# A four-layer macaron kernel: layer 1's second row of keys spread over its half steps, layer 2's expert weights turned ahead of layer 1, and the expert layer's first chunk placed beside the attention's end

## The chip, the core and the metric

The kernel runs on one core of a Trainium2 chip. A core has a matrix engine (TensorE, PE in the profile), a vector engine (VectorE, DVE), an engine for activations and copies (ScalarE, ACT), a general engine (GpSimd, POOL), a queue that issues transfers (SyncE, SP) and 16 DMA engines. Each engine takes its instructions from a queue of its own, in order, and waits on semaphores for the others. The metric is the device time of one execution in microseconds (us), lower being better.

## The reference

The whole model is a residual stream x of 1024 tokens (two rows of 512) with 256 features. Each of four layers is "half an FFN, an attention, half an FFN", each on a layernormed x. The parts that the change touches are the attention of layer 1, and the FFN of layer 2 that follows it:

```python
# layer 1 attention: keys are kept by importance, per row; 16 heads of 16
importance = (x @ Wi + bi)[..., 0]
threshold = sorted_desc[:, tidx][:, None]            # tidx = int(512 * 0.2) = 102
sparse_mask = maximum(importance > threshold, top_32)
q = (x @ Wq + bq)
k = (x @ Wk + bk) * mask
v = (x @ Wv + bv) * mask
out = softmax(q @ k / 4) @ v                          # a masked key keeps a zero score
x = x + out @ Wo + bo
...
# layer 1 FFN: x @ binarized(W).T + bias, taken half
# layer 2 FFN: eight experts, the best one of each token, its gate as weight
probs = softmax(xt @ wg)
out = onehot(argmax(probs)) * gate  combined over  einsum('nh,eoh->neo', xt, W) + b
x = x + 0.5 * out
```

## The kernel before

The kernel runs its stages one after the other: layer 0 with its routed experts, layer 1, and so on. Tokens are held as NC = 8 chunks of 128, four chunks (CB = 4) to a row; features as KD = 2 halves of 128. All operands are 32-bit floats. Matmuls are counted in passes in the trace, two passes to a matmul of this type. A tile framework writes the queues: it puts each engine's instructions in an order by its own estimates unless a block is wrapped in `in_order(tail, engines)` (line 230), which ties the listed engines' instructions to the order in which the code gives them. Tiles come from pools with a fixed number of buffers; a tile waits until the earlier holder of its buffer has been read. PSUM, which receives the matmuls' results, has eight banks.

**Layer 1** (`l1`, line 1382 on) keeps four banks for the scores (`score`). The other four are first one pool of four buffers (`a1m`), then four single buffers (`a1n`): t0 and t1 for transposed probabilities, o for the attention's output, and mm for everything else. Its steps:

- *Front.* `warm(psM, 18)` issues 18 matmuls on constants, 36 passes (L259). For each chunk, `pair` (L1424) adds two routed experts' results, which the y transfers (L861) bring; `sum_products` (L1430, ps_add) adds the rest, and `turn_x`, `back_products`, `back_out` do the half FFN; `measure` and `norm` the layernorm ahead of attention. After chunk 1, `bqs` (L1648), the scaled query bias, is computed on DVE.
- *Row 0's keys.* `importance` (L1474), `own`, `own_out` (L1488), then `ranks(b, cc)`: for one chunk, how many tokens stand above each of its tokens (L1494 on DVE and its sum L1495 on ACT) and which tie (L1498 on DVE). `places` (L1511, L1514) makes a 0/1 matrix from the ranks, `crowd` (L1557, px) multiplies by it so that at most 128 kept keys stand together, `crowded` (L1567) copies the result, `cut_product` and `cut_out` count those used. `key_products` and `keys_out` (L1580, L1592, L1595) make kT and its two masked copies kb; `value_products` and `vals_out` (L1606, L1610 to L1613) make va; `queries` (L1538) makes qT.
- *The prologue* (L1678 on), in order on PE, ACT and DVE: the row-1 importance, row 0's places, a `warm(psM, 4)`, `crowd(0)` and what follows, `queries(1, m)`, and the row-1 ranks.
- *The loop* over N = 16 half steps n (a chunk c = n // 2, and one half of the heads), L1811 on. `products(n)` (L1707, ps_s) makes scores; `lowered(n)` on DVE takes the row maxima (L1715) and subtracts them (L1717, p); `raised(n)` takes the exponential on ACT; `turn(n)` (L1727) transposes p on PE and evacuates it on ACT; `values(n)` (L1740, po) multiplies by va. One chunk behind follow `take_o`, `turn_o` (L1759), `divide`, `turn_back` (L1775), `project` (L1783, pw), `projected` (L1787), then the second half FFN: `centre_x`, `turn_fx` (L1798), `back_products` (L1453), `back_out` (L1456). In half steps n = 0 to 3 the loop also does row 1's places, crowd, keys and values; `kb(1)` is first used in products(8). After the last `lowered`, `self.lowered` marks that DVE instruction.

**Layer 2's weights** (`l2_weights`, L1855 on) load the eight experts' matrices (L1872, 8 transfers of 256 KB) and the gate and bias, and turn them with 32 transposes on PE (L1878) and eight 128x512 evacuations that alternate between DVE and ACT (`evac`, L225 and L227), in four PSUM buffers. This comes after layer 1 in the code; the framework puts it in gaps of the attention's last part. The big transfers use a shared pool of five weight buffers, tag "w", that layer 0's experts use as well.

**Layer 2's FFN** (`l2_ffn`, L1887 on), all experts for each chunk: `measure`, `turn` (L1932), `gates` (L1942, pl, and a chain of small DVE operations that gives the weights w), `experts(c, e2)` for e2 = 0 to 3 (L1964, ps_y, one whole bank of two experts' outputs, added to x by two DVE operations, L1969), `bias_turn`, `bias` (L1984) and `next_turn` (L1919). Only PE's instructions are held in order. All its PSUM tiles share one pool of eight buffers. It is called a second time later.

Of the kernel before, what the change touches and what calls it, by code (L numbers as in the profile page):

```python
# [18 lines left out]
P = 128  # L19
# [156 lines left out]
class Net:  # L176
# [1195 lines left out]
    def l1(self):  # L1372
# [12 lines left out]
        tidx = min(max(1, int(S * 0.2)), S - 1)  # L1385
        keep_min = 32
        assert max(tidx, keep_min) < P
        HQ = 32
        NQ = P // HQ
        GH = P // DH  # L1390
        NG = NH // NQ
        with ExitStack() as es:
# [132 lines left out]
            def cut_product(b):  # L1525
                nc.tensor.matmul(pxs[b][:, KD, 0:CB], self.ones, cuts[b], start=True, stop=True)
# [21 lines left out]

            pxs = {}

            def crowd(b):

                px = pxs[b] = psM.tile([P, KD + 1, P], F32, tag="mm", name="px")
                for k in range(KD):
                    for cc in range(CB):
                        c = b * CB + cc
                        nc.tensor.matmul(  # L1557
                            px[:, k, :],
                            xn[:, c, k * P : (k + 1) * P],
                            place[:, c, :],  # L1560
                            start=(cc == 0),
                            stop=(cc == CB - 1),
                        )
# [44 lines left out]
            def vals_out(b, xk):  # L1608
                uc = sbe.tile([P, 1], F32, tag="uc", name="uc", bufs=2)
                nc.vector.tensor_scalar(uc, self.c["icol"][:, 0:1], cuts[b], None, ALU.is_lt)  # L1610
                vt = sbe.tile([P, D], F32, tag="vt", name="vt", bufs=2)
                nc.vector.tensor_tensor(vt, pvs.pop(b), bv, ALU.add)
                nc.vector.tensor_scalar(  # L1613
                    vas[b][:, :, 0:DH], vt.rearrange("p (h d) -> p h d", h=NH), uc, None, ALU.mult
                )


            with tc.tile_pool(name="a1m", bufs=4, space=PSUM) as psM:
                self.pending.clear()
# [80 lines left out]
            st, po, outs = {}, {}, {}  # L1700

            def products(n):

                c, m = n // 2, n % 2
                for r in range(NQ):
                    q = slice(r * HQ, (r + 1) * HQ)
                    nc.tensor.matmul(  # L1707
                        score[:, r, m], qT[q, m, c * P : (c + 1) * P], kbs[c // CB][q, m], start=True, stop=True
                    )

            def lowered(n):
                c, m = n // 2, n % 2
                half = score[:, :, m]
                mh = mx[:, c, m * GH : (m + 1) * GH].rearrange("p (r j) -> p r j", j=2)
                nc.vector.tensor_reduce(mh, half, AX.X, ALU.max)  # L1715
                p = st[n] = sb.tile([P, NQ, 2, P], F32, tag="p", name="p", bufs=3)
                nc.vector.tensor_tensor(p, half, mh.unsqueeze(3).to_broadcast([P, NQ, 2, P]), ALU.subtract)  # L1717

            def raised(n):
                nc.scalar.activation(st[n], st[n], AF.Exp)  # L1720

# [87 lines left out]
                    f(k // 2)  # L1809

            with self.in_order({}):  # L1811
                products(0)
                lowered(0)
                for n in range(N + 6):
                    if n < N:
                        raised(n)
                    if n + 1 < N:
                        products(n + 1)
                    if n == 0:
                        places(1)  # L1820
# [12 lines left out]
                    if 0 <= n - 1 < N:  # L1833
# [3 lines left out]
                    within(turn_fx, n - 6)  # L1837
                    if n < N:
                        turn(n)
                    if n == 0:  # L1840
                        crowd(1)
                        cut_product(1)
                    elif n == 1:
                        key_products(1, xk)
                    elif n == 2:
                        value_products(1, xk)
                    within(turn_o, n - 2)
                    within(project, n - 3)
# [3 lines left out]
                        self.lowered = self.last_on("DVE")  # L1852


    @contextmanager  # L1855
    def l2_weights(self):

        nc, tc, a = self.nc, self.tc, self.a
        E = 8
        pre = "L2_ffn_"  # L1860
        with tc.tile_pool(name="f2keep", bufs=1) as keep:
            self.w8T = keep.tile([P, KD, E, D], F32, name="w8T")
            self.b8 = keep.tile([E, D], F32, name="b8")
            self.wg8 = keep.tile([P, KD, E], F32, name="wg8")
            self.into = keep.tile([P, KD, T], F32, name="nxT")
            nc.sync.dma_start(self.wg8, a[pre + "wg"].rearrange("(k p) e -> p k e", p=P))
            nc.sync.dma_start(self.b8, a[pre + "b"])
            with tc.tile_pool(name="f2pm", bufs=4, space=PSUM) as psM:
                for e0 in range(0, E, 4):
                    wn = self.w("w8")[:, : 4 * KD * D].rearrange("p (e c d) -> p e c d", e=4, c=KD)  # L1870
                    for e in range(4):
                        nc.sync.dma_start(wn[:, e], a[pre + "W"][e0 + e].rearrange("(c p) d -> p c d", p=P))  # L1872
                    for k in range(KD):
                        for e2 in range(0, 4, 2):
                            ps = psM.tile([P, 2, KD, P], F32, tag="mm", name="ps_w8")
                            for e in range(2):
                                for c in range(KD):
                                    nc.tensor.transpose(  # L1878
                                        ps[:, e, c, :], wn[:, e2 + e, c, k * P : (k + 1) * P], self.ident
                                    )  # L1880
                            self.evac(
                                self.w8T[:, k, e0 + e2 : e0 + e2 + 2, :].rearrange("p e d -> p (e d)"),
                                ps.rearrange("p e c d -> p (e c d)"),
                            )
            yield

    def l2_ffn(self):  # L1887

# [3 lines left out]
        with ExitStack() as es:  # L1892
            sb = es.enter_context(tc.tile_pool(name="f2", bufs=3))
            st = es.enter_context(tc.tile_pool(name="f2s", bufs=1))
            psM = es.enter_context(tc.tile_pool(name="f2m", bufs=8, space=PSUM))
            ms, xts, ws, wTs, nms = {}, {}, {}, {}, {}
            into, self.into = self.into, None
            self.turned = into
# [59 lines left out]
            def experts(c, e2):  # L1958
                if c < 0:
                    return  # L1960
                xT, w, xc = xts[c], ws[c], self.x[:, c, :]
                ps = psM.tile([P, 2, D], F32, tag="mm", name="ps_y")
                for k in range(KD):
                    nc.tensor.matmul(  # L1964
                        ps, xT[:, k, :], self.w8T[:, k, 2 * e2 : 2 * e2 + 2, :], start=(k == 0), stop=(k == KD - 1)
# [746 lines left out]
```

## Time and profile before

| | us |
|---|---|
| three runs: lowest, median, highest | 1840.1, 1843.48, 1847.05 |
| profiled execution | 1847.1 |
| its span in the trace | 1845.3 |
| busy in the span: PE, DVE, ACT, POOL | 1706.4, 1136.6, 808.8, 951.8 |
| layer 1's first warm-up pass on PE starts | 620.78 |
| first ps_add on PE | 630.23 |
| first products, second products | 686.18, 689.50 |
| last values product | 750.81 |
| layer 2 FFN's first transpose | 764.24 |

The page of the profile gives the busy time of each engine, and the same in slices. The timeline gives for every instruction or run of equal instructions on an engine its start, its duration, engine, line, operation, output and inputs, shapes and count, and in brackets the idle time of that engine before it with what ended the wait. The table of windows gives, for stretches of the span, how busy each engine was, the clock granted to PE (1.00 is full), and what the DMA engines did. Durations of matmuls in the trace include the pipeline's length, so two that follow each other overlap by a little.

### The profile page before, as it was taken

Reading aid. Unit: us, or ns where it says so; the run is one execution under the profiler, and the core shown is the slowest. Engines: PE = TensorE matmul, PEld = TensorE weight load, DVE = VectorE, ACT = ScalarE, POOL = GpSimd, SP = SyncE. Lnnn points to the kernel's source line nnn. Section 1 sums busy time; section 2 is a strip of 40 time slices with the busy share of each in tenths; the row PEclk is TensorE's granted clock in tenths of the full one; section 3 lists DMA queues with packets and bytes.
Section 4 is the critical chain, followed back from the end, with each engine's and each line's share of the span. In section 5 each row is a group of like instructions: output and inputs, shape, how many; then the busy total and the mean of one; then the engine's idle time right before and its main releaser. Section 6 shows DMA issues by size and latency. Waiting matters only on the chain. (4 is left out here: it accounts for less than half of the span.)

```text
span 1845.3 us, 29511 instructions
## 1 busy us (share of the span) xinstructions
PE 1706.4 (92%) x10342; PEld 1228.5 (67%) x10342; DVE 1136.6 (62%) x2945; ACT 808.8 (44%) x1399; POOL 951.8 (52%) x974
## 2 busy tenths in 40 slices
PE   6999989999999889998989898799999999999894
PEld 4677756666777657545655476577777777777573
DVE  5533358347433478776867534787777787778533
ACT  1122325421233136315631123678877777777121
POOL 4677646523777441202440263546756657767372
PEclk8999999999999999999989899899999999999897
DMA  9376551052665520102310133444445445443132
GB/s 295 107 229 188 164 193 37 20 176 56 189 182 182 186 75 1 47 1 82 108 33 12 40 103 115 159 140 166 154 140 176 158 140 172 161 149 127 37 117 94
DMA packets 122197, 226.52 MB, mean 123 GB/s; under 512 B 22398, under 2 KB 74988, under 8 KB 121894
## 3 DMA queue, kind: packets, MB, share of 16 engines
q1 hardware_dynamic: 97046, 179.08, 30.1%
q0 software_dynamic: 18944, 42.16, 7.3%
q10 hardware_dynamic: 6032, 3.10, 0.6%
q8 instruction: 91, 1.49, 0.3%
q14 instruction: 84, 0.69, 0.1%
HBM read 195.59 MB, written 41.81 MB: 129 GB/s over the span
## 5 line engine op out<-in xcount | busy, mean ns | idle before, releaser
L645 POOL DMA_INDIRECT xe<-table,sl_get x176 | 183.1, 1040 | 155.1 <-DVE sl_get L617 98.0
L673 PE MATMUL ps_gu<-we,xeT 128*128 128x352 f32 x704 | 225.1, 460 | 0.0
L704 POOL DMA_INDIRECT rows<-ye,sl_put x176 | 176.7, 1004 | 87.9 <-issue 40.2
L2200 DVE SCALAR_TENSOR_TENSOR xc<-pp,L_attn_cols,xc 128x511 f32<-128x511 f32 (+2 forms) x216 | 161.3, 748 | 25.8 <-ACT xc L2196 20.7
L698 PE MATMUL ps_ye<-we,hT 88*128 88x256 f32 x704 | 168.2, 379 | 2.9 <-ACT ye L227 1.6
L678 DVE SCALAR_TENSOR_TENSOR he<-se,xe,ps_gu 128x176 f32<-128x176 f32 x176 | 69.9, 397 | 158.6 <-ACT se L677 154.8
L673 PEld LDWEIGHTS ps_gu<-we,xeT 128*128 128x128 f32 x704 | 126.1, 190 | 55.3 <-DVE xeT L225 1.4
L698 PEld LDWEIGHTS ps_ye<-we,hT 88*128 88x128 f32 x704 | 133.1, 190 | 37.2 <-ACT ye L227 3.6
L2321 DVE SCALAR_TENSOR_TENSOR lm<-lm,jb,top 128x128 f32<-128x128 f32 x576 | 153.5, 342 | 0.0
L2403 POOL TENSOR_TENSOR y<-y,sg 128x512 f32<-128x512 f32 x72 | 91.9, 1276 | 103.5 <-DVE y L2402 102.2
L2433 PE MATMUL yacc<-wt,y 128*128 128x256 f32 x576 | 142.7, 391 | 0.6 <-DVE x L2451 0.3
L677 ACT ACTIVATE se<-ps_gu 128x176 f32<-128x176 f32 x176 | 55.9, 318 | 183.8 <-PE ps_gu L673 181.9
L2348 PE MATMUL pz<-lateT,wt 128*128 128x128 f32 x1024 | 126.2, 276 | 6.3 <-ACT xt L2291 4.1
L2341 POOL TENSOR_TENSOR ce<-ce,CT 128x1024 f32<-128x1024 f32 x54 | 128.0, 2371 | 0.0
L2348 PEld LDWEIGHTS pz<-lateT,wt 128*128 128x128 f32 x1024 | 120.3, 193 | 9.9 <-ACT xt L2291 5.3
L1964 PE MATMUL ps_y<-w8T,xT 128*128 128x512 f32 x256 | 125.0, 618 | 0.0
L2193 PE MATMUL pp<-lateT,wx 128*128 128x512 f32 x256 | 122.1, 600 | 0.8 <-DVE xc L2200 0.8
L2433 PEld LDWEIGHTS yacc<-wt,y 128*128 128x128 f32 x576 | 103.8, 190 | 22.8 <-issue 9.2
L2414 POOL TENSOR_TENSOR sqs<-sqs,sq 128x512 f32<-128x512 f32 x56 | 71.4, 1275 | 85.5 <-ACT sq L2413 85.5
L2376 PE MATMUL py<-lm,xt 128*64 128x128 f32 x1152 | 107.2, 279 | 6.9 <-PE pz L2348 2.1
L2333 DVE TENSOR_TENSOR lm<-lm,M 128x1024 f32<-128x1024 f32 x72 | 87.2, 1215 | 41.9 <-ACT lm L2326 39.4
L2193 PEld LDWEIGHTS pp<-lateT,wx 128*128 128x128 f32 x256 | 48.9, 192 | 57.4 <-issue 52.5
(520 smaller groups left out, 3519.6 us busy)
## 6 DMA issues: line engine op xcount, KB each, us to landing
lm<-rows SPq DMA_DIRECT2D x72, 512.0 KB
ce<-rows SPq DMA_DIRECT2D x54, 512.0 KB
y<-rows SPq DMA_DIRECT2D x16, 768.0 KB
we<-in_L_ffn_w_gate_dram SPq DMA_DIRECT2D x64, 176.0 KB
we<-in_L_ffn_w_up_dram SPq DMA_DIRECT2D x64, 176.0 KB
we<-in_L_ffn_w_down_dram SPq DMA_DIRECT2D x64, 176.0 KB
we<-in_L_ffn_w_dram SPq DMA_DIRECT2D x48, 176.0 KB
wx<-in_L_attn_in_proj_w_dram SPq DMA_DIRECT2D x16, 512.0 KB
```

Of the source, the lines that this page charges most:

```text
L645: nc.gpsimd.indirect_dma_start(xe[:, i, :], None, table, bass.IndirectOffsetOnAxis(get[:, at + j : at + j + 1], 0), bounds_check=T - 1, oo ...
L673: nc.tensor.matmul(pg, xeT[:, k, i * P : (i + 1) * P], wgu[:, :, k], start=(k == 0), stop=(k == KD - 1))
L698: nc.tensor.matmul(py[:, i, :], hT[:, q, i * P : (i + 1) * P], wd[:, q, :], start=(q == 0), stop=(q == 1))
L704: put_rows = nc.gpsimd.indirect_dma_start(rows, bass.IndirectOffsetOnAxis(put[:, at + j : at + j + 1], 0), y[:, i, :], None, bounds_check= ...
L1964: nc.tensor.matmul(ps, xT[:, k, :], self.w8T[:, k, 2 * e2 : 2 * e2 + 2, :], start=(k == 0), stop=(k == KD - 1))
L2193: nc.tensor.matmul(pp, wv[:, k, :], xT[:, k, b * S : (b + 1) * S], start=(k == 0), stop=(k == KD - 1))
L2200: nc.vector.scalar_tensor_tensor(out[:, 3 - w :], pp[:, : S - 3 + w], cw[:, m, w : w + 1], out[:, 3 - w :], ALU.mult, ALU.add)
L2321: nc.vector.scalar_tensor_tensor(k["lm"][:, h, :], k["lm"][:, h, :], jb[:, k["c"], n : n + 1], top, ALU.add, ALU.min)
L2341: nc.gpsimd.tensor_tensor(k["ce"], k["ce"], ct, ALU.mult)
L2348: nc.tensor.matmul(pz[:, m, :], u["wz"][:, kk, m * P : (m + 1) * P], xT[:, kk, c * P : (c + 1) * P], start=(kk == 0), stop=(kk == KD - 1),)
L2376: nc.tensor.matmul(py[i * HP : (i + 1) * HP, m, :], w[:, h * HP : (h + 1) * HP], v[:, h, :], start=(m == 0 and n == 0), stop=(n == len(src ...
L2433: nc.tensor.matmul(yacc[cc // 2][:, cc % 2, :], k["y"][:, m, :], u["wo"][:, m, :], start=(u["g"] == 0 and m == 0 and cc % 2 == 0), stop=(u ...
```

## The change

There are three parts.

1. The loads and turns of layer 2's expert weights move into a method `l2_turned()`, which `l1` calls before anything else. The pool that holds the turned weights stays open through layer 1. In the built program the 32 transposes stand on PE just ahead of the 18 warm-up matmuls; the 256 KB loads stand on SP behind the loads of layer 0's last experts; on DVE, `bqs` stands ahead of DVE's four evacuations.
2. In layer 1's prologue row 0's places and the first half of its crowd come ahead of `own(1)`, the `warm(psM, 4)` is gone, `crowded` copies on ACT, `products(0)` comes ahead of the queries of row 1, and `lowered(0)` is in the prologue. `ranks(1, 1..3)` move into half steps 0 and 1 (on DVE's queue `ranks(1, 1)` still stands between `ranks(1, 0)` and `keys_out(0)`; the other two come after `lowered(1)`). Row 1's places and crowd move from n = 0 to 2, its copy and cut from 1 to 3, its keys from 1 and 2 to 4, its values from 2 and 3 to 4 and 5. The two kb and the one va of row 1 move from DVE to POOL.
3. In layer 2's FFN the eight shared PSUM buffers become four (psM) and four (psY). The first chunk's ps_y takes psM, the other chunks' psY. In the built program PE's queue interleaves the first chunk's FFN with the attention's last steps: values(15), first half of pt(0), turn_fx(5), second half, turn_o(7), back_products(5), gates(0), half of ps_y(0,0), turn_back(7), its other half, project(7), pt(1), the first chunk's bias_turn, half of ps_y(0,1), turn_fx(6), the other half, back_products(6), gates(1), ps_y(0,2), turn_fx(7), bias(0), half of ps_y(0,3), back_products(7), the other half, and then ps_y(1,0).

The diff, cut to its core:

```diff
+        self.l2_turned()
...
-            def crowd(b):
+            def crowd(b, ks=range(KD)):
...
-                nc.vector.tensor_copy(xk, pxs[b][:, 0:KD])
+                nc.scalar.copy(xk, pxs[b][:, 0:KD])
...
-                    nc.vector.tensor_scalar(kbs[b][:, :, j, :], kT, self.c["own"][:, j : j + 1], None, ALU.mult)
+                    (nc.gpsimd if b else nc.vector).tensor_scalar(
+                        kbs[b][:, :, j, :], kT, self.c["own"][:, j : j + 1], None, ALU.mult
+                    )
...
-                nc.vector.tensor_scalar(
+                (nc.gpsimd if b else nc.vector).tensor_scalar(
                     vas[b][:, :, 0:DH], vt.rearrange("p (h d) -> p h d", h=NH), uc, None, ALU.mult
...
                     importance(1)
+                    places(0)
+                    crowd(0, [0])
                     own(1)
-                    places(0)
-                    self.warm(psM, 4)
-                    crowd(0)
+                    crowd(0, [1])
                     chosen(0)
                     own_out(1)
                     cut_product(0)
+                    xk = crowded(0)
                     ranks(1, 0)
-                    xk = crowded(0)
                     key_products(0, xk)
+                    cut_out(0)
                     value_products(0, xk)
-                    cut_out(0)
-                    ranks(1, 1)
                     keys_out(0, xk)
+                    products(0)
+                    vals_out(0, xk)
                     for m in range(KD):
                         queries(1, m)
-                    vals_out(0, xk)
-                    ranks(1, 2)
-                    ranks(1, 3)
+                    lowered(0)
...
-                products(0)
-                lowered(0)
                 for n in range(N + 6):
...
                     if n == 0:
+                        ranks(1, 1)
+                    elif n == 1:
+                        ranks(1, 2)
+                        ranks(1, 3)
+                    elif n == 2:
                         places(1)
                         chosen(1)
-                    elif n == 1:
+                    elif n == 3:
                         xk = crowded(1)
                         cut_out(1)
-                    elif n == 2:
-                        keys_out(1, xk)
-                    elif n == 3:
+                    elif n == 5:
                         vals_out(1, xk)
                     within(projected, n - 4)
                     within(divide, n - 3)
+                    if n == 4:
+                        key_products(1, xk)
+                        keys_out(1, xk)
...
-                    if n == 0:
+                    if n == 2:
                         crowd(1)
                         cut_product(1)
-                    elif n == 1:
-                        key_products(1, xk)
-                    elif n == 2:
+                    elif n == 4:
                         value_products(1, xk)
...
-            psM = es.enter_context(tc.tile_pool(name="f2m", bufs=8, space=PSUM))
+            psM = es.enter_context(tc.tile_pool(name="f2m", bufs=4, space=PSUM))
+            psY = es.enter_context(tc.tile_pool(name="f2y", bufs=4, space=PSUM))
...
-                ps = psM.tile([P, 2, D], F32, tag="mm", name="ps_y")
+                ps = (psY if c else psM).tile([P, 2, D], F32, tag="mm", name="ps_y")
```

`l2_turned` holds the body of the old `l2_weights` unchanged (loads, transposes, evacuations), but for the tile `nxT`, which `l2_weights` still makes, in a pool of its own.

More of the change, by code (lines that the diff above doesn't have):

```diff
@@ L1549, in l1 @@
             pxs = {}
-            def crowd(b):
-                px = pxs[b] = psM.tile([P, KD + 1, P], F32, tag="mm", name="px")
-                for k in range(KD):
+            def crowd(b, ks=range(KD)):
+                if b not in pxs:
+                    pxs[b] = psM.tile([P, KD + 1, P], F32, tag="mm", name="px")
+                px = pxs[b]
+                for k in ks:
                     for cc in range(CB):
@@ L1612, in vals_out, with products, lowered @@
                 nc.vector.tensor_tensor(vt, pvs.pop(b), bv, ALU.add)
-                nc.vector.tensor_scalar(
+                (nc.gpsimd if b else nc.vector).tensor_scalar(
                     vas[b][:, :, 0:DH], vt.rearrange("p (h d) -> p h d", h=NH), uc, None, ALU.mult
                 )
+            st, po, outs = {}, {}, {}
+            def products(n):
+                c, m = n // 2, n % 2
+                for r in range(NQ):
+                    q = slice(r * HQ, (r + 1) * HQ)
+                    nc.tensor.matmul(
+                        score[:, r, m], qT[q, m, c * P : (c + 1) * P], kbs[c // CB][q, m], start=True, stop=True
+                    )
+            def lowered(n):
+                c, m = n // 2, n % 2
+                half = score[:, :, m]
+                mh = mx[:, c, m * GH : (m + 1) * GH].rearrange("p (r j) -> p r j", j=2)
+                nc.vector.tensor_reduce(mh, half, AX.X, ALU.max)
+                p = st[n] = sb.tile([P, NQ, 2, P], F32, tag="p", name="p", bufs=3)
+                nc.vector.tensor_tensor(p, half, mh.unsqueeze(3).to_broadcast([P, NQ, 2, P]), ALU.subtract)
             with tc.tile_pool(name="a1m", bufs=4, space=PSUM) as psM:
@@ L1686, in l1 @@
                     cut_product(0)
+                    xk = crowded(0)
                     ranks(1, 0)
-                    xk = crowded(0)
                     key_products(0, xk)
+                    cut_out(0)
                     value_products(0, xk)
-                    cut_out(0)
-                    ranks(1, 1)
                     keys_out(0, xk)
+                    products(0)
+                    vals_out(0, xk)
                     for m in range(KD):
                         queries(1, m)
-                    vals_out(0, xk)
-                    ranks(1, 2)
-                    ranks(1, 3)
+                    lowered(0)
             psM = es.enter_context(tc.tile_pool(name="a1n", bufs=1, space=PSUM))
[L1700 to L1717, printed above, removed]
             def raised(n):
@@ L1852, in l1, with l2_turned @@
                         self.lowered = self.last_on("DVE")
-    @contextmanager
-    def l2_weights(self):
+    def l2_turned(self):
         nc, tc, a = self.nc, self.tc, self.a
@@ L1860, in l2_weights @@
         pre = "L2_ffn_"
[L1861 to L1885, printed above, removed]
@@ new lines, in l2_turned @@
+        self.l2es = ExitStack()
+        keep = self.l2es.enter_context(tc.tile_pool(name="f2keep", bufs=1))
+        self.w8T = keep.tile([P, KD, E, D], F32, name="w8T")
+        self.b8 = keep.tile([E, D], F32, name="b8")
+        self.wg8 = keep.tile([P, KD, E], F32, name="wg8")
+        nc.sync.dma_start(self.wg8, a[pre + "wg"].rearrange("(k p) e -> p k e", p=P))
+        nc.sync.dma_start(self.b8, a[pre + "b"])
+        with tc.tile_pool(name="f2pm", bufs=4, space=PSUM) as psM:
+            for e0 in range(0, E, 4):
+                wn = self.w("w8")[:, : 4 * KD * D].rearrange("p (e c d) -> p e c d", e=4, c=KD)
+                for e in range(4):
+                    nc.sync.dma_start(wn[:, e], a[pre + "W"][e0 + e].rearrange("(c p) d -> p c d", p=P))
+                for k in range(KD):
+                    for e2 in range(0, 4, 2):
+                        ps = psM.tile([P, 2, KD, P], F32, tag="mm", name="ps_w8")
+                        for e in range(2):
+                            for c in range(KD):
+                                nc.tensor.transpose(
+                                    ps[:, e, c, :], wn[:, e2 + e, c, k * P : (k + 1) * P], self.ident
+                                )
+                        self.evac(
+                            self.w8T[:, k, e0 + e2 : e0 + e2 + 2, :].rearrange("p e d -> p (e d)"),
+                            ps.rearrange("p e c d -> p (e c d)"),
+                        )
@@ L1887, in l2_ffn, with l2_weights @@
+    @contextmanager
+    def l2_weights(self):
+        with self.l2es:
+            with self.tc.tile_pool(name="f2into", bufs=1) as p:
+                self.into = p.tile([P, KD, T], F32, name="nxT")
+                yield
     def l2_ffn(self):
```

## The prediction

> **What bounds the kernel now.** The page's busy line comes first: TensorE (PE) is busy 92% of the 1845.3 us span, VectorE (DVE) 62%, GpSimd (POOL) 52%. The change touches only 617 to 780 us, so its worth is read from that stretch, in the table of windows (in each column busy us, the instruction count in brackets; then the granted clock, 1.00 being full, the DMA share, GB/s):
>
> ```profile
> 620.00:630.00 10.00, 9.22 (x35) 7.92 (x36) 2.36 (x2) 0.00 (x0) 2.33 (x7) 0.80 0.61 198
> 687.00:690.00 3.00, 0.50 (x4) 0.50 (x8) 2.93 (x6) 2.97 (x6) 0.00 (x0) 0.81 0.00 0
> 690.00:696.00 6.00, 6.00 (x35) 5.34 (x30) 2.95 (x6) 2.79 (x4) 0.00 (x0) 0.52 0.00 0
> 757.00:764.00 7.00, 5.31 (x27) 3.60 (x26) 4.17 (x12) 1.92 (x4) 3.44 (x8) 1.00 0.51 150
> 764.00:770.00 6.00, 5.25 (x11) 2.68 (x12) 2.39 (x12) 0.58 (x2) 0.79 (x2) 0.50 0.55 176
> ```
>
> There are three weak places. PE starts layer 1 at 0.80 of its clock; it stands idle for most of 687 to 690 and then works six us at 0.52; it is a quarter idle at the attention's end, and the next FFN then begins at 0.50. The change alters all three. The timeline (start, duration, what it is, in brackets the idle time before it and what ended that) shows each. First the start of layer 1:
>
> ```profile
> 620.78 9.61 PE L259 MATMUL warm<-cst 128*128 128x256 f32 x36 [4.55 <-PEq L839]
> ...
> 624.02 1.67 DVE L1648 TENSOR_SCALAR bqs<-col_L_attn_bq 128x2 f32<-128x2 f32 x1 [7.16 <-issue]
> 630.23 3.62 PE L1430 MATMUL ps_add<-y,cst 128*128 128x256 f32 x16
> ```
>
> The first pair sum (y, 0.69 from 627.29) is ready at 627.98, but ps_add stands behind the warm-up in PE's queue and starts at 630.23, with no idle time in front of it: PE bounds here, by idle work. Then the attention's start, PE's own rows:
>
> ```profile
> 678.21 1.95 PE L1557 MATMUL px<-place,xn 128*128 128x128 f32 x16
> ...
> 682.65 3.60 PE L1538 MATMUL pq<-xT,w 128*128 128x512 f32 x8
> 686.18 0.71 PE L1707 MATMUL ps_s<-kb,qT 32*128 32x256 f32 x8
> 689.50 1.23 PE L1707 MATMUL ps_s<-kb,qT 32*128 32x256 f32 x8 [2.61 <-DVE p L1717]
> 690.66 1.97 PE L1727 MATMUL ps_t<-cst,p 128*128 128x128 f32 x8
> 692.42 3.52 PE L1557 MATMUL px<-place,xn 128*128 128x128 f32 x16
> ```
>
> Ahead of them eight warm-up passes take 1.99 from 676.38. The same crowd matmuls (px) take 1.95 us at 678 and 3.52 at 692, after the idle 2.61. Later the loop is DVE's: in the window 710 to 720 DVE is busy 9.50 of 10 us, of which each half step's lowered() takes 1.23 + 1.23. And the end:
>
> ```profile
> 750.81 0.64 PE L1740 MATMUL po<-pT,va 128*32 128x128 f32 x16
> ...
> 764.24 0.69 PE L1932 MATMUL pt<-cst,xn 128*128 128x128 f32 x2 [0.58 <-DVE x L1456]
> 766.31 3.76 PE L1964 MATMUL ps_y<-w8T,xT 128*128 128x512 f32 x4
> ...
> 775.26 3.70 PE L1964 MATMUL ps_y<-w8T,xT 128*128 128x512 f32 x8
> ```
>
> From the last values product at 750.81 to the FFN's first transpose at 764.24 PE does remnants of attention and the 32 weight transposes. The next chunk's experts begin in the middle of the last row: 775.26 + half of 3.70 = about 777.0.
>
> **A, the weights turned early: a loss of 6.6 us.** The 32 transposes now stand ahead of the warm-up. The w8 loads are issued when experts 27 and 28 free their buffers, about 600, and land before 620; the two small loads go ahead of expert 4's weights on SP, issued at 447.15 and used at 469.9, so they hide (at 8 issues of 0.38 us the worst is 3, within those 20). PE is free at 620.78. A transpose pass costs 0.11 us at full clock (the row of 32 at the end) and 0.21 at half. The first 16 fill four PSUM buffers: 16 x 0.21 = 3.4, to 624.2. The fifth tile needs tile 0's buffer, whose evacuation is a DVE copy that the scheduler queues behind bqs. bqs ran 624.02 to 625.69, after the scatters; one 128x512 copy takes 0.69, so 626.4. The other 16 transposes run to 628.2 (1.76 at 0.11) or 629.9 (0.21). Then 36 warm passes at 0.213 (9.61 us held about 9 at 0.427 and 27 at 0.213): 7.7, up to 9.6 if the clock fell again. So ps_add starts at 635.9 to 639.0, against 630.23: 5.6 to 8.8 later, and I take 6.6, near the warm end. The floor is 3.5, the bare transposes at full clock, if the evacuations do not hold PE. Nothing later absorbs it: the front chunks follow each other every 3.54 us in a PE, DVE, POOL, DVE chain, and the data of y had landed.
>
> **B, the second row's keys later: a gain of 3.3 us.** Removed from PE: the warm 1.99 ahead of crowd(0). Walking each queue with the rows' durations: place(0) is done at 675.57, crowd(0), the importance product (0.4) and the cut products end near 677.9, ACT's copy takes 0.37 where DVE's took 0.42, key products 1.1, kT 0.62, kb 0.64: products(0) at about 681.4 instead of 686.18, since it no longer waits for queries(1) (3.60). lowered(0) ends near 684.7 and the queries fill PE while it runs, so products(1) comes at 685.3 instead of 689.50. That is 4.2 to 4.8. It is partly given back: ranks(1,2) and ranks(1,3), 2 x 1.2 us on DVE, move out of the time when PE did queries and into the loop that DVE bounds. For it the idle 2.61 goes, and with it the half clock (px 3.52 back to 1.95, ps_t 1.97 to 1.04: 2.5, of which DVE's own pace hides some). Moved to POOL and ACT are 2 kb x 0.35, va 0.35 and one later copy of 0.42. The walk reaches products(8) at 714.8 against 718.30, 3.5; I take 3.3. Ends: 1.4 if the clock falls as before, 4.8 if the whole head start is kept. kb(1) on POOL costs 2 x 0.93 by the nearest row (below) but is needed only at products(8), some 10 us later: nothing, or 1 if POOL were a whole chunk late.
>
> ```profile
> L2280 POOL TENSOR_SCALAR wt<-wt,L_attn_cols x8: 920/933/1086, 665.3 to 1141.5; 128x256 f32<-128x256 f32 x8
> L1498 DVE SCALAR_TENSOR_TENSOR cmp<-ib,imp,cst x8: 740/746/1215, 667.4 to 685.8; 128x512 f32<-128x512 f32 x8
> ```
>
> The second row (min/median/max ns) has one instruction of 1215, at 671.79, just beside a POOL addition; that is what POOL work beside the new in-loop ranks could do to DVE: 0.47 each, 1.4 for three, inside my ends. [...]
>
> **C, the FFN's first chunk beside the attention's end: a gain of 9.7 us.** In the changed order PE's queue holds, from values(15) to the second chunk's first ps_y: attention's values 0.6, four pairs of transposes 1.1, turn_o 0.4, projection 0.9, three back products 2.6, together 5.6; the chunk's 4 x 1.72 experts and 2.0 of pt, pl, ct, pb, 8.9. Sum 14.5, to 765.3 at best. The waits that stay are ACT's evacuations behind the one buffer mm (turn_back, project, turn_fx and back_products all use it) and DVE's adds; walking the queues in the new order gives 1.9 of them, so 767.2 instead of 777.0. The 32 transposes (3.5) and 8 evacuations are gone from here, and the FFN starts warm (its first tile 1.9, not 3.76). Gain 9.7; ends 8 (each of the eight DVE steps in the chain 0.2 later) and 11.7. What is late next is x(7), whose last addition moves from 764.18 to 767.0, but its FFN chunk comes 50 us later. The same walk with the old order puts the first transpose at 764.19, where the trace has 764.24. After that the order is the same, 8.47 us a chunk (pl at 772.38 and 780.84).
>
> [...]
>
> **Sum.** -6.6 + 3.3 + 9.7 = 6.4 us gained. The profiled execution took 1847.1 (span 1845.3 and 1.8 around it): 1840.7. It lies 3.6 above the median of the runs, 1843.48, from which 6.4 leaves **1837**. About 0.5% (9.2 us) is what a measurement here can tell from no change; faster is below 1834.3, slower above 1852.7.
>
> **Rivals.**
> - More is gained. If the evacuations run early and the clock holds, A costs 3.5 to 4.5; with B at 4.5 and C at 11 that is 11 to 12: 1832. For it: bqs is the only row that delays the evacuation. Against it: bqs waits for the scatters and stands ahead in DVE's queue.
> - The end does not overlap as intended: one mm buffer and DVE's statistics ahead of the additions stretch the chain, so C is 4: 1843. For it: the old chain of single-buffer steps took 13.4 us from 750.81 to 764.24 with PE only 5.31 of 7 busy. Against it: DVE is 4.17 of 7 busy there.
> - Slower: in the FFN the experts' tiles had eight shared PSUM buffers and now four. Each ps_y waits until the one a chunk earlier has been read. It decides once DVE lags PE by 8.47 - 1.72 = 6.7 us; the row at 777.28 (experts' sums, right behind their products at 777.0) lags under 1.3. The other tiles (pt, pl, ct, pb, pt_nx) have only four too. If either cost 1 us a chunk, over 16 chunks of two calls it is 16: 1853; it is slower from there on.
>
> **Chances.** Forecast 0.52, more gain 0.24, less overlap 0.16, four buffers 0.08. Faster: five sixths of the second, 0.20, and a tail of the first, 0.06: 0.26. Slower: 0.07 from the last. The rest, 0.67, is within 0.5%. The range: all ends good is 3.5 against 4.8 + 11.7, 1830.5; all ends bad 8.8 against 1.4 + 4, 1847. I keep 1829.5 to 1846.
>
> **What would show it.** A: ps_add starts about 6.6 us late with the warm-up right before it. B: no idle over 1 us before products(1), granted clock near 1.00 in the eight us after it, lowered() back to back. C: from values(15) to the second chunk's first ps_y 16.4 us instead of 26.2, clock 1.00, chunks still 8.47 apart. It is wrong if ps_y waits for DVE in the steady chunks, if the clock falls behind the turned weights, or if the in-loop ranks stretch the half steps by more than their 2.4 us.

## The result, and the profile after

The changed kernel takes 1848.03 us (median of 20 runs) against 1842.69 for the kernel before (20 runs): ratio 1.0026, interval 1.0015 to 1.0037, that is 2.8 to 6.8 us slower. A second set (12 runs, e5 below) gave 1.0017, 1.0004 to 1.0029. So it is within 0.5%, but on the other side of no change than forecast, and outside the range of 1829.5 to 1846. The profiled execution took 1847.55 (span 1845.7), as good as the 1847.1 of before's; two single executions do not show the difference, the runs do. So the stages are compared below, and more executions of both.

First the windows that were shown of before, and four others, in the changed kernel (busy us of PE, PEld, DVE, ACT, POOL with counts, then the granted clock, DMA share, GB/s):

```profile
620.00:630.00 10.00, 8.21 (x47) 7.16 (x46) 4.34 (x7) 1.76 (x3) 2.33 (x7) 0.93 0.90 317
660.00:670.00 10.00, 7.71 (x35) 5.26 (x34) 6.40 (x18) 1.12 (x3) 8.98 (x16) 0.79 0.00 1
670.00:680.00 10.00, 9.02 (x26) 4.92 (x24) 6.21 (x16) 3.66 (x9) 4.63 (x8) 0.70 0.01 2
687.00:690.00 3.00, 2.29 (x14) 1.16 (x13) 2.83 (x9) 0.00 (x0) 0.00 (x0) 1.00 0.00 0
690.00:696.00 6.00, 4.58 (x23) 2.12 (x21) 4.14 (x5) 4.61 (x7) 0.00 (x0) 1.00 0.00 0
757.00:764.00 7.00, 7.00 (x33) 4.51 (x32) 5.90 (x24) 2.02 (x7) 3.58 (x9) 1.00 0.00 1
764.00:770.00 6.00, 6.00 (x24) 3.79 (x23) 4.29 (x17) 0.58 (x2) 2.03 (x4) 1.00 0.00 0
830.00:840.00 10.00, 6.58 (x13) 2.67 (x12) 2.71 (x7) 1.43 (x3) 0.78 (x2) 0.66 0.00 0
840.00:850.00 10.00, 10.00 (x41) 6.94 (x40) 4.84 (x11) 1.95 (x5) 0.00 (x0) 0.66 0.00 0
```

Two of the three weak places are mended: full clock from 687 to 696, and PE busy without a break from 757 to 770. But there are new ones, at 660 to 680 and at 830 to 850, where the diff moves nothing. PE's start of layer 1:

```profile
617.23 3.65 PE L1883 MATMUL ps_w<-cst,w 128*128 128x128 f32 x16 [4.05 <-DVEq L839]
622.67 1.97 PE L1883 MATMUL ps_w<-cst,w 128*128 128x128 f32 x16 [1.79 <-DVE w8T L225]
624.48 7.93 PE L259 MATMUL warm<-cst 128*128 128x256 f32 x36
632.25 3.62 PE L1431 MATMUL ps_add<-y,cst 128*128 128x256 f32 x16
```

Sixteen transposes at half clock, 1.79 us of waiting for the evacuation on DVE, sixteen at full clock, the warm-up, and only then ps_add, 15.0 us after PE was free (9.45 before). Next POOL and PE around the last chunk of layer 1's front:

```profile
663.84 0.95 POOL L2292 TENSOR_SCALAR wt<-wt,L_attn_cols 128x256 f32<-128x256 f32 x1 [0.24 <-DVE ln_mv L294]
...
664.94 0.95 POOL L2292 TENSOR_SCALAR wt<-wt,L_attn_cols 128x256 f32<-128x256 f32 x1
665.85 0.57 POOL L303 TENSOR_TENSOR ln_rs<-ln_rs,mhalf 128x1 f32<-128x1 f32 x1
666.40 1.84 POOL L2292 TENSOR_SCALAR wt<-wt,L_attn_cols 128x256 f32<-128x256 f32 x2
```

```profile
664.21 1.13 PE L1454 MATMUL ps_y<-bwT,fxT 128*128 128x256 f32 x4
667.17 0.66 PE L1445 MATMUL pt<-cst,fxn 128*128 128x128 f32 x2 [1.84 <-DVE fxn L307]
```

The same place in the kernel before:

```profile
661.81 0.66 PE L1444 MATMUL pt<-cst,fxn 128*128 128x128 f32 x2 [0.38 <-DVE fxn L307]
...
665.34 3.83 POOL L2280 TENSOR_SCALAR wt<-wt,L_attn_cols 128x256 f32<-128x256 f32 x4
```

wt is a weight of layer 2's attention, scaled on POOL. Before, all four scalings stood behind the last chunk's ln_rs (665.34 on). Now two of them stand ahead of its last step at 665.85, inside the layernorm, and two right behind it, and PE waits 1.84 us for the result instead of 0.38. By the code, part 1 gives two of the shared weight buffers back early: wt is loaded at 646 instead of 658, and the framework puts the scaling earlier too. Then the attention's end, in PE's rows:

```profile
754.55 0.64 PE L1744 MATMUL po<-pT,va 128*32 128x128 f32 x16
...
758.86 1.10 PE L1976 MATMUL ps_y<-w8T,xT 128*128 128x512 f32 x2
...
769.80 2.74 PE L1976 MATMUL ps_y<-w8T,xT 128*128 128x512 f32 x6
```

The overlap is there: the second chunk's experts begin a third into the last row, at 770.7, 16.1 us behind values(15) (26.3 before). And the end of that FFN. There pt_nx turns the last chunk's normed x, pp and pd are the first products of layer 2's attention, pd with only 8 columns, and pst, some 39 us on, is the landmark used below. The idle time is older than the change; first the changed kernel, then the kernel before in the execution of e15:

```profile
833.63 0.69 PE L1931 MATMUL pt_nx<-cst,nxn 128*128 128x128 f32 x2 [2.96 <-DVE nxn L307]
834.78 6.17 PE L2205 MATMUL pp<-nxT,wb 128*128 128x512 f32 x8 [0.46 <-ACT nxT L1932]
840.79 4.63 PE L2145 MATMUL pd<-wb,nxT 128*128 128x8 f32 x32
```

```profile
835.84 0.44 PE L1919 MATMUL pt_nx<-cst,nxn 128*128 128x128 f32 x2 [2.97 <-DVE nxn L307]
836.73 3.70 PE L2193 MATMUL pp<-nxT,wb 128*128 128x512 f32 x8 [0.46 <-ACT nxT L1920]
840.27 3.63 PE L2133 MATMUL pd<-wb,nxT 128*128 128x8 f32 x32
```

The same idle time, the same matmuls, but pp takes 6.17 us instead of 3.70 and pd 4.63 instead of 3.63: half clock (0.66 in the windows above), 64 us behind the second chunk's first ps_y, from which the order is as before.

Stage by stage, in us, from traces that share these landmarks on PE (before and e15 are one kernel, changed and e5 another; e9, e10, e11 are told below):

| from - to | before | e15 | changed | e5 | e10 | e9 | e11 |
|---|---|---|---|---|---|---|---|
| PE free - first ps_add | 9.45 | 9.34 | 15.01 | 14.86 | 14.67 | 14.58 | 9.57 |
| - row 0's importance | 32.03 | 32.04 | 35.38 | 33.69 | 32.01 | 33.71 | 31.65 |
| - row 1's importance | 11.02 | 10.96 | 13.23 | 10.82 | 9.66 | 11.01 | 9.65 |
| - products(8) | 45.02 | 44.98 | 41.31 | 41.32 | 41.59 | 41.31 | 43.21 |
| - values(15) | 32.51 | 32.52 | 32.38 | 32.38 | 32.37 | 32.38 | 32.38 |
| - second chunk's ps_y | 26.27 | 26.24 | 16.11 | 16.12 | 16.12 | 16.12 | 16.12 |
| - last pt_nx | 63.14 | 63.14 | 63.24 | 63.23 | 63.14 | 63.20 | 63.20 |
| - first pst (layer 2's attention) | 38.66 | 38.65 | 45.30 | 45.21 | 44.38 | 38.65 | 38.64 |
| sum | 258.1 | 257.9 | 262.0 | 257.6 | 253.9 | 251.0 | 244.4 |

### The profile page after: what moved, and what is told of

Read it like the earlier page. It is cut to its first block, busy times and chain, and to the rows that moved or that the text cites. A ratio compares the mean times of both kernels' runs of the same rounds, so it can differ in the third digit from the quotient of the medians.

```text
span 1845.7 us, 29481 instructions
## 1 busy us (share of the span) xinstructions
PE 1708.8 (93%) x10334; PEld 1231.0 (67%) x10334; DVE 1134.2 (61%) x2940; ACT 808.5 (44%) x1401; POOL 953.4 (52%) x977
```

## The experiments

My theory after the first trace: the forecast's three terms hold, and two are missing, POOL's new order and more half clock. The rivals: the spread keys or the split buffers lose; or the half clock is luck, alike in both kernels. Runs e1 to e4 were made on a chip on which the kernel before takes 1932.2 us, the others where it takes 1841 to 1843; so whole times are compared as ratios alone. Stages that no edit touches read alike on both chips (products(8) to values(15) takes 32.51 us in e1's trace and in before's). The ratio is always to the kernel before on the same chip.

**e1: part 1 alone.** The kernel before with

```diff
+        self.l2_turned()        # in l1; l2_weights as in the changed kernel
```

> The kernel before with part 1 alone (weights turned ahead of layer 1, eight shared PSUM buffers and old key order kept). My theory: the loss of the change is made at the start of layer 1 (5.6 us later ps_add after PE is free, as in the changed kernel's trace) and by the four wt scalings of layer 2 that now stand on POOL inside the last layernorms (1.8 us and up to 2.2 of half clock behind it); the 32 transposes that go from the attention's end give back at most 3.5. So +4 to +8 us against before. Rival, that the loss comes from the spread keys or the FFN's split buffers: within 2 us of before.

Ratio 1.0047 (1.0023 to 1.0071), 9 us, with an interval of 4.4 to 13.7. Its stages: 14.45 to the first ps_add, then 35.39 and 13.18, where before has 9.45, 32.03, 11.02: 10.5 us lost; from values(15) to the second chunk 22.76 instead of 26.27, 3.5 won; from the last pt_nx to the first pst 42.04 instead of 38.66, 3.4 lost again to half clock. Together 10.4 lost in the trace, a little more than the 4 to 8 expected: part 1 is the loss.

**e2: part 2 alone.** The changed kernel's `l1` without that call, the rest as before.

> The kernel before with part 2 alone (prologue, keys spread, kb and va on POOL). My theory: the changed trace's gain between the second importance product and values(15), 3.8 us, is kept: -3 to -4 us against before. Rival, that the ranks and the second row's keys inside the DVE-bound loop cost more than the head start is worth: 0 to +4 us.

Ratio 1.0003 (0.9976 to 1.003). The expected gain was not found; from row 1's importance to values(15) it is 78.4 us, where before has 77.5. In its trace 6.8 us at half clock fall behind products(1), and products(1) to products(8) take 32.30 us; e3, with the same part 2, has no half clock there and takes 29.40. Its last stage, 44.38 instead of 38.66, holds half clock as the changed kernel's does, though nothing of layer 2 was touched. Whether part 2 by itself is worth anything is not settled by these runs.

**e3: part 1 undone.** The changed kernel with

```diff
-        self.l2_turned()        # in l1
...
     def l2_weights(self):
+        self.l2_turned()
```

> The changed kernel with part 1 undone: the weights are loaded and turned behind layer 1 in the code, as before. My theory: without the loss at the start (5.6) and on POOL (2 to 4) it keeps the 3.8 of the keys and a part of the overlap at the end, some 3 of 10: -5 to -8 us against before, 10 to 13 below the changed kernel. Rival (the start is hidden or the loss is elsewhere): at or above before.

Ratio 0.9949 (0.9922 to 0.9977), 10 us below before on that chip. 10.19 to the first ps_add and 31.82 to row 0's importance: both losses are gone; 21.28 at the end instead of 16.11.

**e4 and e10: POOL's order.** The changed kernel with the scalings held behind the last layernorm of the front:

```diff
+            self.fronts = self.last_on("Pool")       # ahead of the loop's pools in l1
...
+                        with tc.issue_after(self.fronts):
                             nc.gpsimd.tensor_scalar(wo[:, m, :], wo[:, m, :], w, None, ALU.mult)
```

> The changed kernel, but layer 2's four wt scalings on POOL are issued only behind the last layernorm of layer 1's front. My theory: chunk 7's first transpose comes 1.8 us earlier, without the half clock at 668 to 676 it is up to 4: 2 to 4 us below the changed kernel. Rival, that the late front is the clock's alone and not POOL's: 0 to 1 below.

> As e4, the changed kernel with the wt scalings behind the front, once more for a comparison on a chip like that of the changed kernel's runs. My theory: 3.4 us of the front and up to 2 of the half clock behind it are won against the changed kernel: ratio to before 0.998 to 1.000. Rival: the idle time that goes there comes back as half clock later: 1.001 to 1.003.

Ratios 0.9992 (0.9967 to 1.0016) and 0.9997 (0.9978 to 1.0017), against the changed kernel's 1.0026 and 1.0017: 4 to 6 us by the middles, though the intervals touch. The traces agree: the two stages of the front take 41.7 us in e10, 44.5 in e5, 48.6 in the first trace of the changed kernel, of which half clock is a part (none there in e10's trace, 3.4 us in e5's, 13.7 in the first; before has 43.1, with 3.4 us of it). In e10's rows the wait is back at 0.38:

```profile
662.61 1.13 PE L1454 MATMUL ps_y<-bwT,fxT 128*128 128x256 f32 x4
664.12 0.41 PE L1445 MATMUL pt<-cst,fxn 128*128 128x128 f32 x2 [0.38 <-DVE fxn L307]
```

**e5: the changed kernel again.**

> The changed kernel once more, for a second trace beside kernels of the same chip. My theory, from the first trace: from PE free to the first ps_add 15 us, to the first importance product 35.4, values(15) to the second chunk's ps_y 16, last pt_nx of the FFN to the first pst of layer 2's attention anything from 38 to 46, by where the clock's windows of 3.41 us fall on the idle 2.97 us there. Ratio to before 1.000 to 1.005. Rival: the last stage is always 44 to 46 in this kernel and 38 to 40 before.

Ratio 1.0017 (1.0004 to 1.0029). The last stage is 45.21, as in the first trace; with e15 below, two traces of each kernel fit the rival.

**e6: the weights turned in the front.** The loads stay early; the transposes go into PE's idle time, four to a chunk, through the empty score banks, evacuated on ACT, with e4's order on POOL:

```diff
                             turn_x(c - 1)
+                        self.l2_turn(c, score[:, c % NQ])    # 4 transposes, nc.scalar.copy to w8T
```

> The changed kernel with the 32 transposes put into layer 1's front, four behind each chunk's turn_x, into the score banks that stand empty there, evacuated by ACT alone, and with the wt scalings behind the front on POOL. My theory: the first ps_add comes 9.5 us after PE is free, as before (5.5 won), the front keeps its 32 us (3.4 won), the overlap at the end stays: 9 us below the changed kernel, 3 to 6 below before by runs, up to 14 by the trace's stages. Rival: the transposes lengthen the front's chain, 0.3 us a chunk, and half of the gain is gone.

Ratio 0.9968 (0.9954 to 0.9982), 5.9 us below before. 10.07 to the first ps_add, 31.64 to row 0's importance: the transposes lengthen the front by nothing that shows. The last stage is 45.56 here: its half clock is still there.

**e7, e8, e9: the idle time at the FFN's end filled.** Seven warm-up matmuls ahead of the last pt_nx, in e7 on e4's kernel, in e8 on the kernel before, in e9 on the changed kernel:

```diff
                 next_turn(NC - 2)
+                if into is not None:
+                    self.warm(psM, 7)
                 next_measure(NC - 1)
```

> The changed kernel with the wt scalings behind the front on POOL, as in e4, and seven warm-up matmuls (14 passes, 3.0 us) in the idle time ahead of the FFN's last pt_nx. My theory: no half clock in the 15 us behind it, the stage from the last pt_nx to the first pst falls to 38 to 40 us in each run, so that the whole is 3 to 6 us below e4's ratio of 0.999. Rival: the half clock there is not due to the idle time; the stage stays at 44, no gain.

> The kernel before with the same seven warm-up matmuls at the end of layer 2's first FFN. My theory: since its idle 2.97 us is the same, it loses as much to the half clock in most of its runs: 2 to 5 us below before. Rival: the half clock falls there only in the changed kernel: within 1 us of before.

> The changed kernel with nothing but the seven warm-up matmuls ahead of the FFN's last pt_nx. My theory: the half clock behind that idle time is in nearly every run of the changed kernel (45 us to the first pst in both its traces, 38.7 in that of before), so the fill wins 3 to 6 us against the changed kernel where it won nothing in the kernel before: ratio to before 0.998 to 1.000, and a mean granted clock of the runs up from 0.969 by 0.002 or more. Rival (the clock there is luck, alike in both): ratio 1.001 to 1.003 as without the fill.

e7: 0.9956 (0.9938 to 0.9973). e8: 1.0000 (0.9985 to 1.0014). e9: 0.9984 (0.997 to 0.9997). The same fill takes the changed kernel from 1.0017 to 1.0026 down to 0.9984, 6 to 8 us by the middles, and does nothing for the kernel before, whose last stage is 38.66 with the fill as without; e8's expectation fell, e9's held. e9's rows behind the fill are at full clock:

```profile
825.20 3.19 PE L259 MATMUL warm<-cst 128*128 128x256 f32 x14
828.41 0.41 PE L1931 MATMUL pt_nx<-cst,nxn 128*128 128x128 f32 x2
829.28 3.70 PE L2207 MATMUL pp<-nxT,wb 128*128 128x512 f32 x8 [0.46 <-ACT nxT L1932]
832.82 3.63 PE L2147 MATMUL pd<-wb,nxT 128*128 128x8 f32 x32
```

e7 did not reach the 38 to 40 us expected of it, but 42.69: its pp ran at full clock, its pd did not (4.55 us). The trace is of the slowest of its twelve executions (1839.35).

**e11: both together**, e6 with the fill.

> e6 (turns in the front, wt scalings behind it) with the fill of e7. My theory: both gains add: e6's 0.9968 and 3 to 6 us more, ratio 0.993 to 0.995. Rival (fill and front act on the same half clock): 0.9956 to 0.997.

Ratio 0.9907 (0.9885 to 0.9929): 13 to 21 us below before, more than expected. It is the fastest version of the study, on six executions. Its start of layer 1, with a chunk's four transposes between the sums:

```profile
619.03 9.73 PE L259 MATMUL warm<-cst 128*128 128x256 f32 x36 [4.33 <-PEq L839]
628.60 1.89 PE L1431 MATMUL ps_add<-y,cst 128*128 128x256 f32 x8
630.33 0.60 PE L1888 MATMUL ps_s<-cst,w 128*128 128x128 f32 x4
630.77 1.89 PE L1431 MATMUL ps_add<-y,cst 128*128 128x256 f32 x8
```

**e12: the kernel before, 1.28 us later.** `self.warm(psM, 21)` in place of 18 at the start of layer 1. (The windows that it speaks of are explained below.)

> The kernel before with 21 instead of 18 warm-up matmuls at the start of layer 1, which moves all behind by 1.28 us and nothing else. In the trace of before the idle 2.97 us at the FFN's end is cut by a window's boundary of the clock into 1.43 and 1.96 us of work, and the clock stays full; in the changed kernel's it is 1.13 to 1.31 and the clock falls. My theory, that the place of the idle time among the windows decides and is alike from run to run: 3 to 6 us slower than before. Rival, that the windows fall by chance in each run: 1.3 us slower.

Ratio 1.0018 (1.0000 to 1.0036), 0 to 6.6 us: inconclusive between the two, and no test of the theory: the idle time at the FFN's end did not move by 1.28 us among the clock's windows but by 0.27, and an edge still cuts it (1.71 and 1.69 us of matmuls on its two sides, full clock). Its trace has 39.46 us in the last stage, nearly as before.

**e13: part 3 alone**, four and four PSUM buffers in the kernel before.

> The kernel before with part 3 alone, the split PSUM buffers. My theory: the first chunk's ps_y still waits for the 32 transposes and their evacuations, so from values(15) to the second chunk's ps_y 21 to 25 us instead of 26.3, steady chunks unchanged (59.2 us from there to the last ps_y): 0 to 5 us below before. Rival, that four buffers of a kind hold PE up in the steady chunks: slower, with 59.2 grown.

Ratio 0.9976 (0.996 to 0.9991), 1.7 to 7.4 us faster. From values(15) to the second chunk 21.6 us; from there to the FFN's last ps_y 59.20, as in every trace of this study. The split buffers hold nothing up.

**e14: e3 with the fill.**

> e3 (parts 2 and 3, the weights turned late) with the seven warm-up matmuls at the FFN's end. My theory, that the half clock there falls on every kernel unless the idle time is cut in two by a window's boundary: 2 to 5 us below e3's ratio, 0.990 to 0.994. Rival, that only the full overlap brings it: as e3, 0.994 to 0.996.

Ratio 0.997 (0.9954 to 0.9985), no better than e3; the expected 0.990 to 0.994 did not come. Its last stage is 40.34, e3's 40.33, with one window of half clock in the 15 us behind pt_nx in each: in e3 it falls on pp, right behind the idle time, in e14 behind pd, of whose 32 passes 31 start in one window.

**e15: the kernel before, one more trace.**

> The kernel before, for one more trace. If the windows fall by chance: 40 to 45 us from the last pt_nx to the first pst. If before is spared by the place of its idle time: 38.7 again.

1838.75 us in its one execution. The last stage is 38.65, as in the first trace. With e8, where the fill won nothing in twelve runs, it speaks for the place of the idle time and against luck in each execution.

**What decides it.** In all traces here the granted clock changes only at the edges of a grid of 3.413 us, called windows here (29 changes in before's trace and 29 in the changed kernel's); every stretch at half or full clock, but the cut-off last one, is a whole number of such windows. In before and e15 an edge lies 1.0 us ahead of the end of the idle 2.97, so that the windows to both sides hold 1.43 and 1.96 us (1.45 and 1.95 in e15) of matmuls: full clock. In the changed kernel's two traces it lies 0.7 and 0.85 us ahead, and the window before it holds 1.13 and 1.31: half clock for two windows, and again when the 8-column matmuls of pd fill a window. e10 lies on the other side, 1.97 and 1.44, half clock as well.

How the grid cuts pd matters as much. Where its 32 passes are cut into 14 and 18, 16 and 16 or 17 and 15 (before, e15, e8, e9, e11, e3), the clock stays full behind them (pd takes 3.63 us in before, e15 and e9); where 20 to 31 start in one window, half clock follows in ten of eleven traces (23 in the changed kernel, pd 4.63; 22 in e5; 24 in e7, pd 4.55; 31 in e14; the exception is e1 with 22). By these counts the fill mends the first place, and what it wins hangs on the second.

That the place repeats has a reason that some of the traces show. Where on the grid PE stood, in us behind an edge:

| | PE free | first ps_add | row 1's importance | products(1) | values(15) | second chunk | last pt_nx |
|---|---|---|---|---|---|---|---|
| before | 0.16 | 2.78 | 1.45 | 0.61 | 0.48 | 2.86 | 1.15 |
| e15 | 0.39 | 2.90 | 1.53 | 0.68 | 0.52 | 2.87 | 1.16 |
| e8 (before, filled) | -0.41 | 2.49 | 1.29 | 0.44 | 0.39 | 2.80 | 1.15 |

A spread of 0.8 us at the start is 0.41, 0.24, 0.13, 0.07 and 0.01 further on. Each of the first four steps spans one stretch at half clock (in before's trace from 617.21, 661.58, 688.89 and 763.98 on) and nearly halves the spread; the last spans none. My reading, an estimate from the grid and from the px of before (1.95 us at full clock, 3.52 at half): work that starts late in a half window does less of itself at half speed, and the window's end is where the grid has it. The changed kernel's two traces do the same: 1.0 us apart when PE is free, 0.16 at values(15). So in these five traces the kernel's stages, more than chance, put later idle time on the grid, and the change moved it (0.7 and 0.85 us instead of 1.0). It does not hold everywhere. e7 and e10 run the same code up to the fill and are 0.2 us apart at row 1's importance, but 1.7 at values(15): a window with 1.60 us of matmuls brought half clock in e7, at 695.83, and the same window with 1.79 did not in e10. e6 and e11, alike up to the fill, are 0.5 apart at the first ps_add and at values(15) too.

The clock recorded for the timed runs points the same way. Its mean is 0.9717 for before (32 runs), 0.9674 and 0.9688 for the changed kernel (20 and 12), 0.9732 for e9, 0.9777 for e11 (6 runs). One minus the clock, times some 1843 us, is an estimate of the work at full clock that was lost to it: 52.2 us before, 60.1 and 57.5 changed. The difference, 5 to 8 us, is more than the whole loss of 3.1 to 4.8. It is an upper estimate of the time lost, since PE does not bound everywhere: e8's mean of 0.9729 would be 2.2 us less lost than before, and its time is the same. That the changed kernel would be the faster one without its half clock is shown by e9 (0.9984), not by this sum.

## Why the prediction was wrong, point by point

- **A, a loss of 6.6** (5.6 to 8.8): measured 5.4 to 5.6 (15.01 and 14.86 against 9.45 and 9.34). The mechanism is the forecast one: 16 transposes at half clock, a wait for the evacuation behind bqs, 16 at full clock, then 7.93 of warm-up. It is the low end, since the clock stayed full from the second half of the transposes to the warm-up's end (half from 614.50 to 621.33, then full to 638.40). (The high end is mis-added: 629.9 and 9.6 make 639.5, not 639.0; nothing rests on it.)
- **B, a gain of 3.3**: measured 3.7 from row 1's importance to products(8), and the loop kept 3.8 to values(15). products(1) came with the queries ahead of it, as walked. The ranks in the loop were within their price. Part of the gain is the clock's: before's own code takes 43.7 instead of 45.0 in this stage in e12 and e13, with one window of half clock behind products(1) instead of two, and the new code takes 43.1 to 43.2 in e6, e7 and e11, with one window, instead of 41.3. And part 2 alone won nothing that the runs of e2 could show.
- **C, a gain of 9.7**: measured 10.15 in every trace with the overlap.
- **The sum "-6.6 + 3.3 + 9.7 = 6.4" is the step that failed**: its terms hold to 1.1 us, but it had only the stages that the diff names, and put everything between and behind them at nothing.
  - "Nothing later absorbs it: the front chunks follow each other every 3.54 us" took layer 1's front as unchanged. What the early turn frees is missing: two shared weight buffers, with them layer 2's wt loads, and with these four POOL instructions of 3.8 us in and right behind the front's last layernorm. The forecast followed SP's queue past the moved loads, and not POOL's. The two stages of the front became 1.5 us longer than before's in e5 and 5.6 in the first trace, more half clock included; against e10, where POOL's order is undone, they are 2.8 and 6.9 longer.
  - Missing is second the half clock at the FFN's end, 5.7 to 6.9 us in that stage by the five traces with the overlap and without a fill (changed, e4, e5, e6, e10); e9 took it out.
  - With both, the changed kernel's stages add up: -5.5 + 3.8 + 10.15 is 8.4 us won; less 1.5 to 5.6 in the front and 6.6 at the FFN's end, between 0.3 won and 3.8 lost is left. e7, the changed kernel with POOL's order undone and the fill, is 8.1 us below before (5.0 to 11.4), about the 8.4 that the three forecast terms measure.
- **"After that the order is the same, 8.47 us a chunk"**: true up to the last pt_nx (63.2 us in all). "What is late next" should have looked at the next idle time too, not only at x(7).
- The clock: with the same idle time half clock followed in the changed kernel (2.96 us, then pp 6.17) and not in before (2.97 us, then pp 3.70); what the traces point to is the matmul time within one window. Behind a full-clock window with 1.42 us of matmuls or less half clock followed in all 168 cases in the 17 traces (7 of them in before's trace, 8 in the changed kernel's); from 1.43 to 2.0 us it followed in 5 of 10 cases in before's trace and in 2 of 5 in the changed kernel's.
- Rivals, in short: "more is gained" did not come about; "the end does not overlap" is false (16.1); "four buffers" is false (e13, 59.20). The sign "if the clock falls behind the turned weights" named the clock, but at the wrong place.
- Of the measured loss of 3.1 to 4.8, the eight stages of the two traces give, by their sums, -0.4 and 3.9. The rest, some 2 us, stays open; it is within what single executions differ by: behind the first pst the two traces of before take 966.4 and 962.3 us, those of the changed kernel 966.5 and 966.8.

The parts add up, by their ratios: part 1 +0.47%, part 2 +0.03%, part 3 -0.24%, together +0.26%, which is what the whole showed; with intervals of a quarter per cent each, the close agreement is partly luck. The stage from values(15) to the second chunk does not add up so: part 1 alone won 3.5 there, part 3 alone 4.6, both with part 2 10.15.

## What to carry to other kernels

Work moved out of the way of one stage frees buffers, and a scheduler fills these with work from later layers: after a move, read the order of every queue, the one that the diff does not name above all. Here the move to an earlier place paid only where PE was idle: the same 32 transposes cost 5.5 us ahead of the warm-up and less than 1 us inside the front (e6, 10.07 and 31.64 against 9.45 and 32.03). And when a change shortens a kernel, look where the remaining idle times fall among the clock's windows (2.97 us here, with half clock behind it or not). A fill like the one of e7 to e9 is cheap to try and not sure to help: it was worth 6 to 8 us in the changed kernel and nothing in the kernel before or in e3.

## What the runs showed of the hardware

- The granted clock changed only on a grid of 3.413 us. In the 17 traces every full-clock window with 1.42 us of matmuls or less was followed by half clock (168 cases). Above that it went both ways: in before's trace half clock followed the windows of 1.46 us at 941.48 and of 1.77 at 760.57, and not those of 1.43 at 835.66 and of 1.92 at 750.33. So the edge is not sharp in matmul time.
- 32 matmuls of 8 columns filled 3.63 us of PE's busy time in two windows at full clock (e9, 16 and 16). Where most of them fell in one window, half clock followed too: 23 of 32 in the changed kernel, in a window with 3.42 us of busy time from 839.78 on (4.63 in all), and 24 of 32 in e7 (4.55, behind a pp of 3.70).
- Three executions that started up to 0.8 us apart on that grid were 0.01 us apart 220 us later (before, e15, and e8, the kernel before with the fill); others drifted apart (e7 and e10, from 0.2 to 1.7 us).
- The tie count on DVE (128x512) took 0.74 to 0.75 us in 13 of its 16 instructions in the traces of before and of the changed kernel. It took 1.22 at 671.79 of before's and 1.21 at 678.55 of the changed kernel's, where an addition of 0.90 us on POOL had started 0.24 us ahead of it (671.55 and 678.31), and 0.96 at 667.40 of before's, beside wt's scaling on POOL. With POOL busy beside it for 0.77 us it took no longer at 669.99 of before's (0.74) and at 676.75 of the changed kernel's (0.75).
